# Batch 0 of the first layer: its operands built earlier among its adjacency pieces, and its attention put beside its own preparation

## The chip, the cores and the metric

One Trainium2 chip, one of its cores. The metric is device time in microseconds (us) of one execution of the whole program, from three runs of the kernel before; beside them stands one execution taken by the hardware profiler. The engines of the core are named as in the profile: PE (TensorE) multiplies matrices, DVE (VectorE) and ACT (ScalarE) work element by element, POOL (GpSimd) and SP (SyncE) here mostly issue transfers. Each engine takes its own instructions in a fixed order and waits on semaphores of the others.

## What is computed

Four graph layers over 16 graphs of 1024 nodes with 128 features, each inside `x = layernorm(x + layer(x, adj))`. The change touches only the first layer, for each graph `b`:

```
h       = x @ W.T + W_b                          # 1024 x 128
e       = (h A) h.T ;  e = e + e.T               # 1024 x 1024
att     = softmax(where(adj > 0, e, -9e15), axis=1) * adj
h_prime = relu(att @ h)
c       = sigmoid([x, h_prime] @ gate_w.T + gate_b)
layer   = c * x + (1 - c) * h_prime
```

The later layers (a dilated adjacency with three aggregation steps and batch norms, a second attention, a two-step graph convolution) are not touched.

## The kernel before, in words

The program runs `fast_kernel`; `general_kernel` stands behind a flag for inputs that the fast one does not cover.

**First layer, operands.** The scores are folded: with `M0 = W.T (A + A.T) W` (built from the raw weights at the start, with the column `nu` from the bias), `e` needs only `xT` (x turned, 128 x 1024) and `G = -(M0.T xT) + nu`. `hn` is h by rows, from `xT` and the turned weight `l0WT`. The raw weights (`l0W`, `l0A`, `l0As`, `l0AW`, `l0b`) lie in a pool `l0_raw` on the left side of SBUF; it is closed when `M0` and `nu` exist, and the pool `l0_work`, opened next on the same side, takes over the space. The first tile in it is `xn` of batch 0.

**Preparation, `before(s, b)`.** It loads `xn`, then eight pieces of the adjacency (`it` = 0 to 7), each 128 rows x 1024 (512 KB) into `an`, of which there are three buffers. A piece is cast to fp8 on ACT (the "cast", into `carry`, with the row sums); DVE checks the part right of the diagonal (`chk<-an`); PE turns the blocks up to the diagonal (`pt<-identb,carry`, `it + 1` of them) and DVE compares them with the piece (`chk<-pt,an`), after which the `an` buffer is free. Among the pieces the operands are built: `xT` in the step of piece 2, `G` and the gate part `gx` in that of piece 4, `hn` in that of piece 5. Last, POOL issues the write of the fp8 adjacency to memory (`adj_d<-carry`).

**Attention, `attention(s, b)`.** For each of eight row tiles `jt`: ACT makes the mask (`msk`), PE the scores in two halves (`pmm`, two buffers in PSUM), DVE adds the mask and takes the minimum (`em`, two buffers), ACT takes the exponential with its sum, DVE the reciprocal and the scaled rows `hs`; one round later PE accumulates `acc += hs.T em` in two halves. Row tile `jt` needs the cast of piece `jt` and the columns `jt` of `G`, `xT` and `hn`. Below, e0 stands for the scores of tile 0, acc0 for its accumulation.

**Finish, `after(s, b)`.** Relu, the gate, the mix with x, the layernorm, and the write of x1.

**Order of the work.** The three are generators; `in_rounds` steps those that are due in each round and a `yield n` sets a stream's next turn n rounds on. That fixes the program's order; a scheduler then fixes the order of each engine's queue from it, and may move an instruction ahead of others in the program. In the kernel before, `before(0)` is put in alone; then for each `b` one call of `in_rounds` takes `before(b + 1)`, `attention(b)` and `after(b - 1)` together. The gate bias `gbh` is halved on DVE ahead of all of it.

Of the kernel before, what the change touches and what calls it, by code (L numbers as in the profile page):

```python
# [17 lines left out]
OP = mybir.AluOpType  # L18
# [621 lines left out]
def fast_kernel(ctx: ExitStack, tc: tile.TileContext, t: dict, out: bass.AP, flag: bass.AP):  # L640

    nc = tc.nc
    B, N, D = t["x"].shape
# [43 lines left out]
    def nat(ap):  # L687
        return ap.rearrange("(t p) d -> p t d", p=P)
# [7 lines left out]
    def column(pool, src, name):  # L696
        v = pool.tile([P, 1], F32, name=name)
        nc.sync.dma_start(v, bass.AP(tensor=src.tensor, offset=src.offset, ap=[[1, P], [1, 1]]))
        return v

    def matrix(pool, src, name, bufs=1):
        v = pool.tile([P, P], F32, name=name, bufs=bufs)
        nc.sync.dma_start(v, src)
        return v

    def transposed(pool, psum, src, name, tag="tr"):
        v = pool.tile([P, P], F32, name=name)
        p = psum.tile([P, P], F32, name="wtr", tag=tag)
        nc.tensor.transpose(p, src, identf)
        nc.vector.tensor_copy(v, p)  # L710
        return v
# [103 lines left out]
    def in_rounds(streams):  # L815

        due, r = [0] * len(streams), 0
        while any(streams):
            for i, s in enumerate(streams):
                if s is not None and due[i] <= r:  # L820
                    pause = next(s, 0)
                    if pause == 0:
                        streams[i] = None
                    else:
                        due[i] = r + (pause or 1)
            r += 1

    def symmetric(pool, psum, A, name, tag="tr"):
        As = pool.tile([P, P], F32, name=name)
        p = psum.tile([P, P], F32, name="wtr", tag=tag)  # L830
        nc.tensor.transpose(p, A, identf)
        nc.vector.tensor_add(As, A, p)
        return As
# [57 lines left out]
    ps_a = ending.enter_context(tc.tile_pool(name="l0_pa", bufs=1, space=PSUM, reuse_waits="tile"))  # L891
    ps_h = ending.enter_context(tc.tile_pool(name="l0_ph", bufs=2, space=PSUM, reuse_waits="tile"))

    with tc.tile_pool(name="l0_raw", bufs=1) as raw:
        W0 = matrix(raw, t["L0_gnn_W_w"], "l0W")
        W0T = transposed(wts, ps_h, W0, "l0WT", "h")
        As0 = symmetric(raw, ps_h, matrix(raw, t["L0_gnn_A"], "l0A"), "l0As", "h")
        AW = raw.tile([P, P], F32, name="l0AW")
        p = ps_h.tile([P, P], F32, name="wtr", tag="h")
        nc.tensor.matmul(p, As0, W0, start=True, stop=True)  # L900
        nc.vector.tensor_copy(AW, p)
        M0 = wts.tile([P, P], F32, name="l0M")
        p = ps_h.tile([P, P], F32, name="wtr", tag="h")
        nc.tensor.matmul(p, W0, AW, start=True, stop=True)
        nc.vector.tensor_copy(M0, p)
        nu = wts.tile([P, 1], F32, name="l0nu")
        p = ps_h.tile([P, 1], F32, name="wtr", tag="h")
        nc.tensor.matmul(p, AW, column(raw, t["L0_gnn_W_b"], "l0b"), start=True, stop=True)
        nc.vector.tensor_scalar(nu, p, -1.0, None, op0=OP.mult)
# [6 lines left out]
        nc.sync.dma_start(gw[:, :, 0], t["L0_gnn_gate_w"].rearrange("o (h d) -> d (o h)", d=P))  # L916
    gb = row_bcast(wts, t["L0_gnn_gate_b"], 1, "l0gb")
    gbh = wts.tile([P, 1], F32, name="l0gbh")
    nc.vector.tensor_scalar(gbh, gb, 0.5, None, op0=OP.mult)
    nbig = wts.tile([P, 1], F32, name="l0nbig")  # L920
    nc.vector.memset(nbig, BIG)

    def before(s, b):

        s.xn = work.tile([P, NT, P], F32, name="xn", bufs=3)
        nc.sync.dma_start(s.xn, nat(t["x"][b]))
        yield 1
        for it in range(NT):
            c = b * NT + it
            an = early.tile([P, N], F32, name="an", bufs=3)  # L930
            nc.sync.dma_start(an, t["adj"][b][it * P:(it + 1) * P, :])
            nc.scalar.activation(Y[b][:, it, :], an, AF.Copy, accum_out=deg[:, c:c + 1], saturate=False)  # L932

            chk = early.tile([P, N], FP8, name="chk")
            done = (it + 1) * P
            if done < N:
                nc.vector.scalar_tensor_tensor(chk[:, done:], an[:, done:], 0.0, an[:, done:], op0=OP.is_gt,
                                               op1=OP.not_equal, accum_out=other[:, b, it:it + 1], saturate=False)
            for h in range(it // 4 + 1):
                js = range(4 * h, min(4 * h + 4, it + 1))  # L940
                k = slice(js[0] * P, (js[-1] + 1) * P)
                pt = ps_h.tile([P, 512], F32, name="pt", tag="h")
                for i, jt in enumerate(js):
                    nc.tensor.matmul(pt[:, i * P:(i + 1) * P], Y[b][:, jt, it * P:done], identb, start=True, stop=True)
                nc.vector.scalar_tensor_tensor(chk[:, k], pt[:, :k.stop - k.start], 0.0, an[:, k], op0=OP.is_gt,
                                               op1=OP.not_equal, accum_out=other[:, b, 7 + it + 4 * h:8 + it + 4 * h],
                                               saturate=False)
            if it == 2:
                s.xT = work.tile([P, N], F32, name="xT", bufs=2)
                for p, c, _ in turned(ps_h, s.xn):  # L950
                    nc.scalar.copy(s.xT[:, c], p)
            elif it == 4:
                s.G = work.tile([P, N], F32, name="G", bufs=2)
                for p, c in products(ps_h, (M0, s.xT)):
                    nc.scalar.activation(s.G[:, c], p, AF.Identity, scale=-1.0, bias=nu)
                pz = gates(ps_h, early.tile([P, N], FP8, name="chk").bitcast(F32), (gw[:, 0, :], s.xT))
                s.gx = small.tile([P, NT], F32, name="gx")
                nc.vector.tensor_copy(s.gx.rearrange("p (q t) -> p q t", t=2), pz[:, :, :, 0])
            elif it == 5:
                s.hn = work.tile([P, N], F32, name="hn")  # L960
                for p, c, blocks in halves(ps_h):
                    for i, k in enumerate(blocks):
                        nc.tensor.matmul(p[:, i * P:(i + 1) * P], s.xT[:, k * P:(k + 1) * P], W0T, start=True, stop=True)
                    nc.vector.tensor_add(tiles3(s.hn[:, c]), tiles3(p), b0[:, None, :].to_broadcast([P, 4, P]))
            yield 2
        nc.gpsimd.dma_start(adj8_d[b], Y[b].bitcast(F32))

    def attention(s, b):
        s.acc = ps_a.tile([P, N], F32, name="acc")

        def weigh(jt, hs, em):
            for h in range(H2):
                c = slice(h * 512, (h + 1) * 512)
                nc.tensor.matmul(s.acc[:, c], hs, em[:, c], start=(jt == 0), stop=(jt == NT - 1))  # L974

        for jt in range(NT):
            js = slice(jt * P, (jt + 1) * P)
            c = b * NT + jt
            mn = mx0[:, c:c + 1]
            msk = work.tile([P, N], BF16, name="msk", bufs=2)  # L980
            nc.scalar.activation(msk, Y[b][:, jt, :], AF.Identity, scale=-BIG, bias=nbig)  # L981
            e = wide_matmul(ps_w, s.G[:, js], s.xT)
            em = work.tile([P, N], F32, name="em", bufs=2)
            nc.vector.tensor_tensor_reduce(em, e, msk, 1.0, 3.0e38, op0=OP.add, op1=OP.min, accum_out=mn)  # L984
            sm = small.tile([P, 1], F32, name="sm")
            nc.scalar.activation(em, em, AF.Exp, scale=-1.0, bias=mn, accum_out=sm)  # L986
            rs = small.tile([P, 1], F32, name="rs")
            nc.vector.reciprocal(rs, sm)
            hs = small.tile([P, P], F32, name="hs")
            nc.vector.tensor_scalar(hs, s.hn[:, js], rs, None, op0=OP.mult)  # L990
            yield
            if jt:
                weigh(*late)
            late = jt, hs, em
            yield
        weigh(*late)
        yield
# [23 lines left out]
        yield  # L1021

    state = [Batch() for _ in range(B)]
    in_rounds([before(state[0], 0)])
    for b in range(B):
        streams = []
        if b < B - 1:
            streams.append(before(state[b + 1], b + 1))
        streams.append(attention(state[b], b))
        if b:  # L1030
            streams.append(after(state[b - 1], b - 1))
        in_rounds(streams)
# [225 lines left out]
    with ExitStack() as ph:  # L1258
# [230 lines left out]
        before = None  # L1489
# [5 lines left out]
        for l in range(3):  # L1495
# [42 lines left out]
            before = step  # L1538
# [7 lines left out]
    with ExitStack() as ph:  # L1546
# [7 lines left out]
        W2T, b2, As2, gw, gb, nbig, blcol, Wl = l2.W2T, l2.b2, l2.As2, l2.gw, l2.gb, l2.nbig, l2.blcol, l2.Wl  # L1554
# [247 lines left out]
        state = l2.state  # L1802
# [63 lines left out]
```

## Time and profile before

| what | us |
|---|---|
| three runs, lowest, median, highest | 2731.83, 2735.02, 2736.03 |
| the profiled execution, its own time | 2734.11 |
| its span, first to last instruction | 2732.4 |
| PE, DVE, ACT busy in the span | 2552.2, 2108.6, 1977.0 |
| first layer's attention, first score product to the lull of PE | 28.57 to about 630 |

In the profile L12 is line 12 of the kernel. A line of the timeline gives start, duration, engine, line, operation and `out<-in`, with a count where several were merged, and in brackets the idle time before it and what ended it. SPq and POOLq are the queues from which transfers are issued, and the time shown for one of them is that of the issue; the landing comes later. A matmul line at f32 is counted as two per 512 columns.

### The profile page before, as it was taken

The page shows a single profiled execution, that of the slowest core. Times are in us where ns is not written, and L with a number is a line of the kernel's source. Part 1 is how long each engine was busy: PE and PEld are TensorE (multiplying, and loading weights), DVE is VectorE, ACT ScalarE, POOL GpSimd, SP SyncE. Part 2 cuts the span into 40 slices and gives each one's busy share as a digit, 9 for nine tenths or more (in the row PEclk, how much of TensorE's full clock was granted, in tenths as well). Part 3 has the DMA queues.
Part 4 walks back from the last instruction along what each step waited for, and adds up shares of the span by engine and source line. Part 5 has one row for each costly group of instructions (what it writes and reads, how often), then busy time and mean ns, then how long its engine had stood idle before and what let it go on. Part 6 is the DMA issues. An engine that isn't in the chain of part 4 may idle for free.

```text
span 2732.4 us, 41821 instructions
## 1 busy us (share of the span) xinstructions
PE 2552.2 (93%) x15048; PEld 1688.8 (62%) x15048; DVE 2108.6 (77%) x5650; ACT 1977.0 (72%) x3188; POOL 317.1 (12%) x287
## 2 busy tenths in 40 slices
PE   7999999994899888998999998999999999999986
PEld 3444444442666657887778887456666666666655
DVE  5887778875999986776678877577787787787785
ACT  6888889873888786666655543777777777777773
POOL 0000000003000001121112123001010010001001
PEclk9999999996999999999999999999999999999998
DMA  5455445430000042233356655101222211111100
GB/s 189 162 169 171 165 167 177 157 114 23 2 2 2 2 183 96 94 108 124 132 203 224 254 205 211 39 24 62 70 77 73 90 62 62 62 62 62 46 24 25
DMA packets 120810, 285.38 MB, mean 104 GB/s; under 512 B 12305, under 2 KB 65425, under 8 KB 113425
## 3 DMA queue, kind: packets, MB, share of 16 engines
q1 hardware_dynamic: 101280, 203.33, 22.4%
q0 software_dynamic: 19312, 79.28, 7.5%
q8 instruction: 121, 1.98, 0.3%
q14 instruction: 97, 0.79, 0.1%
HBM read 202.72 MB, written 79.82 MB: 103 GB/s over the span
## 4 chain that ended last, share of the span: by engine, by line
PE 62%; DVE 16%; issue 9%; POOL 5%; ACT 4%; DMA 3%; SPq 0%; POOLq 0%; ACTq 0%; DVEq 0%
PE acc L974 8%; PE ph L1618 8%; PE pmm L724 8%; PE acc L1678 7%; PE ph L766 6%; PE acc L1306 5%; PE ph L759 4%; PE pmm L1690 3%; POOL rn L745 2%; PE ph L1605 2%; PE ph L1432 2%; DVE mid L1097 2%; POOL ln_rstd L745 1%; PE s L1144 1%; DVE keep L1148 1%
## 5 line engine op out<-in xcount | busy, mean ns | idle before, releaser
L745 POOL TENSOR_TENSOR ln_rstd<-ln_rstd,mhalf 128x8 f32<-128x8 f32 (+1 forms) x68 | 108.3, 1592 | 1347.6 <-DVE ln_rstd L742 879.7
L974 PE MATMUL acc<-em,hs 128*128 128x512 f32 x512 | 260.1, 607 | 1.9 <-DVE past L1075 1.3
L724 PE MATMUL pmm<-xT,G 128*128 128x512 f32 x512 | 261.8, 604 | 0.0
L1678 PE MATMUL acc<-ex,hs 128*128 128x512 f32 x512 | 248.9, 596 | 7.4 <-DVE hs L1705 4.5
L801 ACT ACTIVATE xn<-xn,ln_nb,ln_rstd 128x128 f32<-128x128 f32 x512 | 204.6, 481 | 70.3 <-DVE ln_nb L799 70.3
L1306 PE MATMUL acc<-a,lo 128*128 128x512 f32 x768 | 240.4, 398 | 15.3 <-DVE lo L1273 15.3
L1306 PE MATMUL acc<-a,hi 128*128 128x512 f32 x768 | 241.4, 399 | 3.8 <-ACT hi L1272 3.6
L986 ACT ACTIVATE em<-em,mx 128x1024 f32<-128x1024 f32 x128 | 146.4, 1144 | 63.5 <-DVE mx L984 63.0
L1698 ACT ACTIVATE ex<-em,mn 128x1024 f32<-128x1024 f32 x128 | 146.8, 1147 | 44.6 <-DVE mn L1695 43.9
L984 DVE CUSTOM_DVE_ANT_0 em<-pmm,msk 128x1024 f32<-128x1024 f32 x128 | 156.0, 1219 | 27.0 <-PE pmm L724 26.4
L1306 PEld LDWEIGHTS acc<-a,lo 128*128 128x128 f32 x768 | 144.3, 190 | 52.2 <-DVE lo L1273 22.6
L1690 PE MATMUL pmm<-G,hT 128*128 128x512 f32 (+3 forms) x416 | 175.3, 523 | 0.1
L1695 DVE CUSTOM_DVE_ANT_0 em<-pmm,msk 128x1024 f32<-128x1024 f32 x128 | 155.3, 1214 | 24.4 <-PE pmm L1692 22.3
L1306 PEld LDWEIGHTS acc<-a,hi 128*128 128x128 f32 x768 | 144.1, 191 | 34.1 <-ACT hi L1272 4.6
L1157 ACT ACTIVATE carry<-pc,negone 128x1024 fp8e4<-128x1024 f32 x128 | 140.8, 1114 | 27.0 <-PE pc L1156 21.7
L932 ACT ACTIVATE carry<-an 128x1024 fp8e4<-128x1024 f32 x128 | 134.4, 1050 | 21.7 <-DMA an<-in_adj 20.7
L981 ACT ACTIVATE msk<-carry,l0nbig 128x1024 bf16<-128x1024 fp8e4 x128 | 145.4, 1137 | 0.0
L1618 PE MATMUL ph<-A,hi 128*128 128x512 f32 x512 | 143.1, 420 | 1.2 <-DVE zn L1607 0.7
L1686 ACT ACTIVATE msk<-A,nbig 128x1024 bf16<-128x1024 fp8e4 x128 | 144.1, 1136 | 0.0
L1678 PEld LDWEIGHTS acc<-ex,hs 128*128 128x128 f32 x512 | 88.7, 190 | 76.8 <-issue 54.6
L1295 ACT CAST a<-A 128x1024 fp32r<-128x1024 fp8e4 x96 | 99.1, 1050 | 50.9 <-PE acc L1306 50.9
L1295 ACT CAST a<-carry 128x1024 fp32r<-128x1024 fp8e4 x96 | 99.3, 1049 | 47.6 <-PE acc L1306 47.4
(319 smaller groups left out, 6237.4 us busy)
## 6 DMA issues: line engine op xcount, KB each, us to landing
an<-in_adj SPq DMA_DIRECT2D x128, 512.0 KB, 3.6
adj_d<-carry POOLq DMA_DIRECT2D x16, 1024.0 KB, 4.2
A<-dil_d SPq DMA_DIRECT2D x16, 1024.0 KB, 5.6
rdeg<-rdeg_d SPq DMA_DIRECT2D x32, 512.0 KB, 3.8
A<-adj_d SPq DMA_DIRECT2D x16, 1024.0 KB, 4.8
ag_d<-ag POOLq DMA_DIRECT2D x24, 512.0 KB, 5.0
ag<-ag_d SPq DMA_DIRECT2D x24, 512.0 KB, 5.0
xn<-in_x SPq DMA_DIRECT2D x16, 512.0 KB, 4.3
```

What stands on the lines that cost most here:

```text
L724: nc.tensor.matmul(p[:, h * 512:(h + 1) * 512], lhsT, rhs[:, h * 512:(h + 1) * 512], start=True, stop=True)
L745: nc.gpsimd.tensor_tensor(r, r, mhalf[:, :n], op=OP.pow)
L766: nc.tensor.matmul(p, W, x[:, c], start=(i == 0), stop=(i == len(pairs) - 1))
L801: nc.scalar.activation(r[:, k.start + i, :], r[:, k.start + i, :], AF.Identity, scale=rstd[:, i:i + 1], bias=nb[:, i:i + 1])
L974: nc.tensor.matmul(s.acc[:, c], hs, em[:, c], start=(jt == 0), stop=(jt == NT - 1))
L984: nc.vector.tensor_tensor_reduce(em, e, msk, 1.0, 3.0e38, op0=OP.add, op1=OP.min, accum_out=mn)
L1295: nc.scalar.copy(a, A[:, 2 * i:2 * i + 2, c])
L1306: nc.tensor.matmul(acc, part[:, jt, :], pieces[h * NT // 2 + i][:, j, :], start=(jt == 0 and p == 0), stop=(jt == NT - 1 and p == 1))
L1618: nc.tensor.matmul(p, part[:, jt, :], A[jt][:, c], start=(jt == 0 and i == 0), stop=(jt == NT - 1 and i == 1))
L1678: nc.tensor.matmul(s.acc[:, c], hs, ex[:, c], start=(jt == 0), stop=(jt == NT - 1))
L1690: nc.tensor.matmul(e[:, c], s.hT[:, js], s.G[:, c], start=True, stop=True)
L1695: nc.vector.tensor_tensor_reduce(row, e, msk, 1.0, 0.0, op0=OP.add, op1=OP.min, accum_out=mn)
```

## The change

1. The pool of the raw weights goes on the right side of SBUF, so that `l0_work` takes no space from it.
2. For batch 0 alone, `xT` is built in the step of piece 0 (before: piece 2), `G` and `gx` in that of piece 1 (before: 4), `hn` in that of piece 2 (before: 5). For all other batches they stay in the steps of pieces 2, 4 and 5.
3. The first call of `in_rounds` takes `before(0)`, `attention(0)` from round 8 on, and `before(1)` from round 16 on. Piece `it` of batch 0 has its turn in round `1 + 2 it`, tile `jt` of its attention in round `8 + 2 jt`, and piece `it` of batch 1 in round `17 + 2 it`. The loop over `b` then starts with `b = 1`.
4. The instruction that halves the gate bias stands after that first call.

```diff
@@ -891,7 +891,7 @@
-    with tc.tile_pool(name="l0_raw", bufs=1) as raw:
+    with tc.tile_pool(name="l0_raw", bufs=1, side="right") as raw:
...
@@ -916,7 +916,6 @@
     gbh = wts.tile([P, 1], F32, name="l0gbh")
-    nc.vector.tensor_scalar(gbh, gb, 0.5, None, op0=OP.mult)
...
@@ -945,18 +944,18 @@
-            if it == 2:
+            if it == (2 if b else 0):
                 s.xT = work.tile([P, N], F32, name="xT", bufs=2)
...
-            elif it == 4:
+            elif it == (4 if b else 1):
                 s.G = work.tile([P, N], F32, name="G", bufs=2)
...
-            elif it == 5:
+            if it == (5 if b else 2):
                 s.hn = work.tile([P, N], F32, name="hn")
...
@@ -1021,8 +1020,9 @@
     state = [Batch() for _ in range(B)]
-    in_rounds([before(state[0], 0)])
-    for b in range(B):
+    in_rounds([before(state[0], 0), chain([8], attention(state[0], 0)), chain([16], before(state[1], 1))])
+    nc.vector.tensor_scalar(gbh, gb, 0.5, None, op0=OP.mult)
+    for b in range(1, B):
         streams = []
         if b < B - 1:
             streams.append(before(state[b + 1], b + 1))
```

More of the change, by code (lines that the diff above doesn't have):

```diff
@@ L951, in before @@
                     nc.scalar.copy(s.xT[:, c], p)
-            elif it == 4:
+            if it == (4 if b else 1):
                 s.G = work.tile([P, N], F32, name="G", bufs=2)
```

## Prediction

> **What bounds the kernel now.** I read the page's slices first, then a table of busy time by stretch, then the timeline of the first 45 us, then the waits of the transfer queue.
>
> ```profile
> span 2732.4 us, 41821 instructions
> PE   7999999994899888998999998999999999999986
> DVE  5887778875999986776678877577787787787785
> ACT  6888889873888786666655543777777777777773
> ```
>
> The first layer fills slices 0 to 8 of 68.3 us each. PE is at 9 in all but the first, so this stage ends when PE has done its work, and what counts at the head is how long PE stands idle. By stretch (columns: length, then busy PE, PEld, DVE, ACT, POOL, clock, DMA share, GB/s):
>
> ```profile
> 0.00:14.00 14.00, 3.28 (x12) 2.32 (x13) 5.13 (x30) 6.68 (x9) 1.08 (x8) 1.00 0.40 131
> 14.00:29.00 15.00, 9.18 (x35) 4.38 (x33) 5.70 (x20) 6.09 (x13) 0.00 (x0) 1.00 0.87 275
> 29.00:45.00 16.00, 14.74 (x71) 7.71 (x70) 12.91 (x39) 11.04 (x19) 0.71 (x1) 1.00 0.60 203
> 45.00:60.00 15.00, 15.00 (x68) 7.47 (x67) 10.21 (x37) 14.56 (x26) 0.00 (x0) 1.00 0.45 143
> 300.00:400.00 100.00, 100.00 (x425) 49.62 (x424) 82.25 (x274) 90.47 (x156) 9.15 (x9) 1.00 0.51 170
> ```
>
> PE idles 10.7 + 5.8 + 1.3 = 17.8 us up to 45 us, and then not at all (later rows are like the last). ACT at 90% and DVE at 82% have slack. So a microsecond of PE idleness saved in the head is a microsecond of the program. Why is PE idle?
>
> ```profile
> 7.04 0.15 DVE L919 TENSOR_SCALAR l0gbh<-l0gb 128x1 f32<-128x1 f32 x1 [4.13 <-DMA l0gb<-in_L_gnn_gate_b]
> 8.46 1.09 DVE L937 SCALAR_TENSOR_TENSOR chk<-an 128x896 fp8e4<-128x896 f32 x1 [1.27 <-DMA an<-in_adj]
> 10.98 0.27 DVE L832 TENSOR_TENSOR l0As<-l0A,wtr 128x128 f32<-128x128 f32 x1
> 13.53 0.38 SPq L926 DMA_DIRECT2D xn<-in_x  x1
> 17.88 1.94 PE L759 MATMUL ph<-identf,xn 128*128 128x128 f32 x8 [3.08 <-DMA xn<-in_x]
> 23.85 3.78 PE L766 MATMUL ph<-xT,l0M 128*128 128x512 f32 x4 [0.95 <-DVE chk L945]
> 28.57 1.14 PE L724 MATMUL pmm<-xT,G 128*128 128x512 f32 x2
> ```
>
> DVE's constants queue behind the first piece's check, so l0As is late; xn is issued only when the raw weights' space is free; xT, G and the first scores follow in a chain. Once attention runs, the engines pace one another:
>
> ```profile
> 37.90 1.06 ACT L932 ACTIVATE carry<-an 128x1024 fp8e4<-128x1024 f32 x1 [3.25 <-DMA an<-in_adj]
> 38.96 1.13 ACT L986 ACTIVATE em<-em,mx 128x1024 f32<-128x1024 f32 x1
> 40.09 1.13 ACT L981 ACTIVATE msk<-carry,l0nbig 128x1024 bf16<-128x1024 fp8e4 x1
> 42.60 1.22 DVE L984 CUSTOM_DVE_ANT_0 em<-pmm,msk 128x1024 f32<-128x1024 f32 x1
> ```
>
> A piece that lands late stops ACT. The waits of SP's own queue to 60 us (in all, times, longest) and the transfers' time to landing say why it may:
>
> ```profile
> SPq L931 <- DVE chk L945: 51.5, 15, 12.8
> SPq L926 <- DVE l0AW L901: 6.9, 1, 6.9
> DMA to landing us min/median/max: 3.4/4.7/5.8
> ```
>
> Three an buffers; each new load waits for DVE's last check of an old piece, then takes 4.7 us.
>
> **What the Trainium skill says.** *PSUM — Partial Sum Buffer*, section "Engine vs sequencer instructions": engine queues are strict FIFO, matmuls complete in program order. The trace agrees: xn's wait held the an loads behind it to 14.34. *DMA: Bandwidth & Descriptors*, "Anatomy of one DMA — SWDGE (gpsimd) path": about 2.0 us fixed plus bytes over 436 GB/s, an estimate of 3.2 us for 512 KB; the trace's 4.2 for xn (13.53 to 17.8) and 4.7 for an are longer, on SP's queue, and I use those. *TensorE: Matmul & The Clock Gate*, "What's actually happening": PE runs at half rate until busy for some 3.4 us. The trace agrees in kind: the four M0 products take 3.78 us at 23.85 and 1.94 us at 51.65, though the clock column says 1.00 at both.
>
> **The change, part by part.** I walk the built instruction order of the changed kernel with durations above. Pace (start to start) is what queues up: cast 1.05, exp 1.13, mask 1.04, em 1.14; on PE scores 1.72 and accumulation 1.77 per tile, hn 1.8.
>
> *Raw pool, loads.* In the built order SP issues xn of batch 0 at the place of the first an (4.14), then three an, then xn of batches 1 and 2, then piece 3. xn lands at about 8.4. The three an follow at 9.7, 11.0, 12.3: before, they landed from 8.4 on, and 1.3 us is 512 KB at the 418 GB/s seen from 8 to 10 us. So the pieces pay 1.3 us. The extra xn loads (2.6 us) delay nothing: piece 3's load waits for the check of piece 0 (12.8) and lands near 17.2, and its cast is due at 18.3.
>
> *gbh.* The scheduler puts it back where it was on DVE, waiting to 7.04. Value 0; bounds 0 to 0.15 either way.
>
> *M0.* The constants now precede the first check: l0As at 7.19 + (10.98 - 9.48) = 8.7. But that check (9.7 to 10.75) stands ahead of l0AW, so M0 comes at 12.2, not 13.6.
>
> *xT, G, first scores.* Turns of xn 12.3 to 14.25 (as slow as before), one slot of piece 1, M0 products from 14.6: 3.78 us if cold, 1.94 if warm. PE has by then been nearly continuously busy since 11.1, so I take 3.0; gate products 0.8; first scores at 18.4 (bounds 17.4 and 19.4), 10.2 us before 28.57. PE has done 9.4 us of work by then (3.0 up to M0, from the 3.28 of the first row; 0.7 for the turns of pieces 0 and 1; 1.9; 3.0; 0.8): 9.0 us idle.
>
> *What is late next.* At 28.57 the old kernel had six casts and five pieces' checks done; the new one at 18.4 has three and two. The rest now shares ACT and DVE with attention. New waits, by queue:
> - DVE: em of tile 0 waits for e0 (20.2); behind it the check of piece 2, done at 23.0. SP's load of piece 5 waits for that: issued 23.1, landed 27.5 (4.4 us; ends 3.4 and 5.8). Its cast fits just in time.
> - Piece 3's check, behind em of tile 1 and both halves of hn, ends at 26.95: piece 6 lands at 31.45. ACT has nothing in front of that cast from 28.55, and exp of tile 2 is queued behind it. On PE the turns of piece 6 wait, with acc1's second half behind: **1.5 us idle**.
> - acc7 waits for hs of tile 7, behind exp7 and DVE's checks of pieces 3 and 4 of batch 1: **1.0 us**.
> - The gate turns of batch 1 wait for ACT's copy, behind the cast of piece 6 and the relu: **1.0 us**.
> - Small ones (piece 5, acc5): 0.3. POOL's 1 MB write, freed by cast 7 at about 34.8 instead of 31.5, now meets the loads of batch 1's pieces 1 and 2; 0.5 for that (0 to 2; it is not free, for nothing hides a late cast here). Nothing waits for POOL itself; further on its x1 write goes ahead of the next batch's adjacency write, with no reader near: 0.
>
> Sum after 18.4: 4.3 us. The alone stretch of batch 1's pieces 4 to 7, which the rounds suggest, costs nothing more: the built order fills it with batch 1's scores, G and hn.
>
> *Sum.* Idle PE after: 9.0 + 4.3 = 13.3, against 17.8: **4.5 us saved**. Cross-check by content: the walk has e0 of batch 1, acc7 and the gate turns done at 61.7 + 0.5; the old trace reaches that content at 70.95 less 3.2 us of work further on (hn and two pieces' turns), 67.75: 5.5 us. From batch 3 on the orders are the same, PE is full in both, and the rest moves as one. Profiled: 2734.1 - 4.5 = 2729.6 (span 2732.4 to 2727.9, 1.7 around it). The median of the runs is 0.9 above the profiled execution: 2735.0 - 4.5 = **2730.5**.
>
> **Rivals.**
> *A, the stalls are hidden.* PE turns warm early and loads land in 3.4 us, so only about 1.3 us of idleness is left, as in 29 to 45 now: with scores at 17.4, 8.0 + 1.3 = 9.3 idle, 8.5 saved, 2726.5. For: the page's min of 3.4; PE is busy on end from 11.1. Against: a median of 4.7 with the same number of loads in flight.
> *B, slower: the ring of three an buffers behind in-order DVE.* Every piece from 5 of batch 0 to 4 of batch 1 (8 of them) stalls PE as piece 6 does. At 5.8 us to landing, 1.4 more than I took, each adds 1.4 x 8 = 11.2 idle: 13.3 + 11.2 = 24.5, 6.7 slower, 2741.7. It decides from 4.5 / 8 = 0.6 us extra per piece, that is from 5.0 us to landing. For: ACT already waited 3.25 us for one piece. Against: after piece 6 the walk has most loads landing before ACT reaches their cast.
> *C, nothing.* The gain is eaten on the way to batch 3, PE waits up to 17.8 in sum: 2735. For: ACT at 90% has to catch up three casts. Against: its slack of 10% is 3 us per 30.
> That the change does not do what it says is excluded by the built order: xn heads the loads and scores come before piece 2's turns.
>
> **How the numbers follow.** A measurement of this kernel tells about 0.2% (5.5 us) from no change, so my 4.5 sits just inside. Main forecast 0.50 (2728 to 2733); A 0.24; C 0.16; B 0.10. Faster by over 0.2%: A and a third of the main case (0.18): 0.42. Slower: most of B, with a little of C: 0.10. Same: 0.48. Range 2725.5 to 2737: A's end and a little under it, and C with the runs' spread, leaving out B and tails.
>
> **What would show it.** First scores (pmm) near 18.4 and the M0 products near 14.6; xn issued at about 4.1; piece 6's cast with a wait for its load near 31 and PE idle before its turns; PE's idle sum to 65 us near 13.3. Wrong if first scores come after 21, if idle PE appears past 70 us, or if loads take over 5.0 us.

## The result and the profile after

| | kernel before | changed kernel |
|---|---|---|
| median of the runs (lowest to highest) | 2733.41 (2730.95 to 2736.03), 9 runs | 2726.49 (2723.03 to 2730.03), 9 runs |
| the profiled execution, its own time | 2734.11 | 2723.06 |
| its span | 2732.4 | 2721.3 |

The ratio is 0.9976, with a 95% interval of 0.9966 to 0.9985: the median of the changed kernel is 6.9 us lower (4.1 to 9.3 by the interval). The forecast was 2730.5, 4.5 us faster. In the runs of the experiments below, one execution of e3_alone, of 3651.69 us at a granted clock of 0.66, is left out. The two profiled executions differ by more, 11.1 us in span. So there are two questions: is the head's gain what the steps said, and where does the rest come from?

The page's first line and three rows of its slices, in the kernel after:

```profile
span 2721.3 us, 41812 instructions
PE   8999999994899889998999998999999999999986
DVE  6788777875999986776678877577877878787785
ACT  7888889873888786666655544777777777777773
```

PE's first slice is at 8 where it was at 7, and DVE and ACT are busier in slice 0. By stretch (length, then busy PE, PEld, DVE, ACT, POOL, clock, DMA share, GB/s):

```profile
0.00:14.00 14.00, 4.50 (x16) 3.29 (x17) 6.04 (x32) 4.86 (x8) 1.08 (x8) 1.00 0.70 216
14.00:29.00 15.00, 14.54 (x68) 7.67 (x67) 8.58 (x29) 12.54 (x19) 0.00 (x0) 1.00 0.47 137
29.00:45.00 16.00, 15.35 (x58) 6.86 (x56) 13.83 (x42) 13.31 (x22) 0.71 (x1) 1.00 0.78 258
45.00:60.00 15.00, 13.43 (x52) 6.14 (x51) 6.21 (x22) 13.61 (x22) 0.00 (x0) 1.00 0.42 139
300.00:400.00 100.00, 100.00 (x416) 49.77 (x415) 79.57 (x263) 90.08 (x156) 9.49 (x9) 1.00 0.53 172
```

Length less busy PE gives 9.50, 0.46, 0.65 and 1.57 us of idle PE, and the rows after these add 0.84 (60 to 75 us), 0.55 (90 to 105) and 0.47 (120 to 200). The sum is 14.0, where the kernel before had 17.8. The stretch of 14 to 29 us was 5.8 idle and is now almost full; 45 to 60 was full and now is not. The timeline shows the start of the chain:

```profile
4.14 0.43 SPq L925 DMA_DIRECT2D xn<-in_x  x1
7.10 0.15 DVE L1024 TENSOR_SCALAR l0gbh<-l0gb 128x1 f32<-128x1 f32 x1 [4.15 <-DMA l0gb<-in_L_gnn_gate_b]
8.67 0.28 DVE L832 TENSOR_TENSOR l0As<-l0A,wtr 128x128 f32<-128x128 f32 x1
10.10 1.09 DVE L936 SCALAR_TENSOR_TENSOR chk<-an 128x896 fp8e4<-128x896 f32 x1 [1.15 <-DMA an<-in_adj]
12.73 1.96 PE L759 MATMUL ph<-identf,xn 128*128 128x128 f32 x8
15.36 3.08 PE L766 MATMUL ph<-xT,l0M 128*128 128x512 f32 x4 [0.46 <-ACT xT L950]
18.94 1.98 PE L724 MATMUL pmm<-xT,G 128*128 128x512 f32 x4
```

xn is issued 9.4 us sooner, PE has no idle time just ahead of xn's turns (they now follow the weights' small products and the turn of piece 0), and the first scores start at 18.94 instead of 28.57. The main waits of ACT and PE after that:

```profile
30.97 1.06 ACT L931 ACTIVATE carry<-an 128x1024 fp8e4<-128x1024 f32 x1 [2.60 <-DMA an<-in_adj]
33.97 1.06 ACT L931 ACTIVATE carry<-an 128x1024 fp8e4<-128x1024 f32 x1 [0.72 <-DMA an<-in_adj]
35.17 0.23 PE L943 MATMUL pt<-identb,carry 128*128 128x128 bf16 x1 [0.56 <-ACT carry L931]
52.72 0.22 PE L943 MATMUL pt<-identb,carry 128*128 128x128 bf16 x1 [0.57 <-DVE chk L944]
53.94 1.12 PE L766 MATMUL ph<-xT,l0M 128*128 128x512 f32 x2 [1.00 <-DVE chk L944]
68.32 1.06 ACT L931 ACTIVATE carry<-an 128x1024 fp8e4<-128x1024 f32 x1 [2.34 <-DMA an<-in_adj]
69.53 0.23 PE L943 MATMUL pt<-identb,carry 128*128 128x128 bf16 x1 [0.84 <-ACT carry L931]
101.42 1.10 PE L973 MATMUL acc<-em,hs 128*128 128x512 f32 x2 [0.55 <-DVE hs L989]
```

How much of the head's gain survives is read from marks. POOL's power of `ln_rstd` belongs to a batch's normalisation, after its attention: for batch 0 it starts at 92.68 before and 88.24 after (4.4 us sooner), for the fourth at 205.30 and 200.71 (4.6), for the fourteenth at 580.45 and 576.12 (4.3). The first instruction after the first layer that both kernels have on POOL is the power of the degrees. Before:

```profile
627.96 20.73 POOL L1183 TENSOR_TENSOR deg<-deg,mhalf 128x128 f32<-128x128 f32 x1 [5.87 <-DVE deg L1182]
```

and after:

```profile
623.52 20.74 POOL L1183 TENSOR_TENSOR deg<-deg,mhalf 128x128 f32<-128x128 f32 x1 [5.87 <-DVE deg L1182]
```

The lead at this mark, called the degree mark below, is **4.44 us**. Up to 992 us the two traces keep it within 0.3 us. It then grows to 11.1 at 1848 us, in a stage whose instructions are the same in both, and stays there to the end.

### The profile page after: what moved, and what is told of

Its sections match the earlier page's. It is cut to its first block, busy times and chain, and to the rows that moved or that the text cites. A ratio compares the mean times of both kernels' runs of the same rounds, so it can differ in the third digit from the quotient of the medians.

```text
span 2721.3 us, 41812 instructions
## 1 busy us (share of the span) xinstructions
PE 2547.0 (94%) x15048; PEld 1683.6 (62%) x15048; DVE 2108.4 (77%) x5650; ACT 1977.4 (73%) x3188; POOL 317.0 (12%) x287
## 4 chain that ended last, share of the span: by engine, by line
PE 58%; DVE 17%; issue 7%; POOL 5%; ACT 5%; DMA 2%; POOLq 0%; ACTq 0%; DVEq 0%; SPq 0%
PE ph L1618 8%; PE acc L1678 7%; PE acc L973 6%; PE pmm L724 6%; PE acc L1306 6%; PE ph L766 6%; PE ph L759 3%; PE pmm L1690 3%; PE ph L1605 2%; POOL rn L745 2%; PE ph L1432 2%; POOL ln_rstd L745 2%; DVE mid L1097 1%; ACT q L1145 1%; PE s L1144 1%
```

## The experiments

Two theories were put to the test. The first: the head's gain is less idle PE, because xn is there early and xT and G are made beside the first pieces. Its rivals: the order of the rounds makes the gain, or ACT's pace at the pieces hides all of it, or (the prediction's slower rival) the ring of three an buffers decides. The second: what the profiled pair shows beyond 4.4 us is a matter of where the TensorE clock's half-rate windows fall. Its rival: the change shortens the later stage too.

All times are in us; "idle" is the sum of PE's idle time to 400 us; the medians are of runs made together, with the kernel before run beside them on the same chip. First scores, idle time and mark are those of one profiled execution each.

| run | first scores | idle | degree mark | median, kernel before | ratio, 95% interval |
|---|---|---|---|---|---|
| before | 28.57 | 17.8 | 627.96 | | |
| changed | 18.94 | 14.0 | 623.52 | 2726.49, 2733.41 | 0.9976 (0.9966 to 0.9985) |
| after_again | 19.83 | 14.7 | 624.56 | 2725.29, 2731.18 | 0.9979 (0.9970 to 0.9989) |
| e1_left | 24.90 | 18.5 | 629.14 | 2732.55, 2732.39 | 0.9998 (0.9990 to 1.0006) |
| e2_right | 26.15 | 15.0 | 626.03 | 2730.39, 2732.39 | 0.9991 (0.9983 to 0.9999) |
| e3_alone | 18.92 | 14.4 | 626.08 | 2725.68, 2732.39 | 0.9967 (0.9954 to 0.9980) |
| e4_late_ops | 25.87 | 18.7 | 628.89 | 2732.04, 2732.39 | 0.9996 (0.9990 to 1.0003) |
| e9_m0 | 19.30 | 13.4 | 623.46 | 2730.47, 2732.45 | 0.9992 (0.9983 to 1.0001) |
| e10_xt | 20.09 | 13.7 | 624.50 | 2730.15, 2732.45 | 0.9990 (0.9984 to 0.9997) |
| e11_dve | 17.85 | 12.3 | 622.85 | 2724.96, 2731.18 | 0.9976 (0.9964 to 0.9987) |
| e6_an4 | 20.40 | 13.7 | 621.19 | 2725.50, 2732.45 | 0.9978 (0.9968 to 0.9988) |
| e12_dve4 | 19.00 | 11.1 | 620.32 | 2724.21, 2731.18 | 0.9973 (0.9962 to 0.9984) |
| e7_an2 | 18.75 | 31.2 | 665.85 | 2765.24, 2732.45 | 1.0119 (1.0103 to 1.0134) |

The two executions of the changed kernel show what one reading is worth: 18.94 and 19.83 for the first scores, 14.0 and 14.7 idle, 623.52 and 624.56 at the mark. A difference of about 1 us between two kernels is therefore not read as an effect. Idle time saved and lead at the mark agree within 1.0 us in all runs but three: e3_alone, e6_an4 and e7_an2, which are taken up below.

**e1_left: the raw weights back on the left side.**

```diff
-    with tc.tile_pool(name="l0_raw", bufs=1, side="right") as raw:
+    with tc.tile_pool(name="l0_raw", bufs=1) as raw:
```

> The changed kernel, but the raw weights stay on the left side, where xn's space is only free after they are used. Theory (the gain is PE idleness saved in the head, and the early xn is its first cause): xn is issued near 13.5 us again instead of 4.14, its turns start near 17.9 and the M0 products near 20, first scores at 22 to 24 instead of 18.94; three to four of the 4.4 us of lead that the changed kernel has at the degree reciprocal (line 1183: 623.52 against 627.96) are lost, so that mark lies at 626.5 to 627.5; idle PE up to 75 us near 17. Rival (the order of the rounds alone carries the gain): the mark stays at 623.5 to 624.5. Second theory, on the other 6.7 us of the profiled pair: the time from this mark to the end follows the microseconds that the clock record shows at half clock there (20.5 before, 6.8 after) at half a microsecond each, whatever the head does; its rival: the time after the mark is set by the order of the head.

The timeline of this kernel:

```profile
13.57 0.38 SPq L925 DMA_DIRECT2D xn<-in_x  x1
17.82 1.94 PE L759 MATMUL ph<-identf,xn 128*128 128x128 f32 x8 [3.84 <-DMA xn<-in_x]
24.90 1.12 PE L724 MATMUL pmm<-xT,G 128*128 128x512 f32 x2
```

xn is late again. The first scores come later than expected (24.90, not 22 to 24), and the mark is not some 1 us better than before, as the theory had it, but 1.2 us worse; the medians are equal to 0.2 us. Without the early xn the rest of the change gives nothing, although its scores still start 3.7 us sooner than before. The rival, that the order of the rounds alone carries the gain, is out. Earlier scores alone are thus no gain; idle PE is 18.5. (The 20.5 and 6.8 us at half clock in the expectation are what is left without the windows that both executions have in the same places. From the mark to the end it is 130.1 and 116.4 in all; the difference of 13.7 is the same.)

**e2_right: the kernel before, with only the raw weights on the right side.**

```diff
-    with tc.tile_pool(name="l0_raw", bufs=1) as raw:
+    with tc.tile_pool(name="l0_raw", bufs=1, side="right") as raw:
```

> The kernel before, with only the raw weights moved to the right side. Theory: xn is issued near 4.1 us and lands near 8.4, but xT and G keep their place at pieces 2 and 4 and attention its place behind the preparation, so first scores come at 26 to 28.6 against 28.57, and the degree mark at 626 to 628 (lead 0 to 2). Rival (the early xn carries the gain): lead 3.5 to 4.5, mark at 623.5 to 624.5. For the rest of the time: half a microsecond per microsecond at half clock after the mark, as in the other runs.

```profile
4.14 0.43 SPq L926 DMA_DIRECT2D xn<-in_x  x1
21.43 3.78 PE L766 MATMUL ph<-xT,l0M 128*128 128x512 f32 x4 [0.76 <-DVE chk L945]
26.15 1.30 PE L724 MATMUL pmm<-xT,G 128*128 128x512 f32 x2
```

xn comes at the same 4.14 as in the changed kernel, but the products of G have kept their place among the pieces and start at 21.43. The lead is 1.9 at the mark, where that rival asked for 3.5 to 4.5, and 2.0 in the medians (0.3 to 4.6 by the interval). So the early xn by itself is a part of the gain, about half of it or less, and by the mark not all of it.

**e4_late_ops: the changed kernel with xT, G and hn at pieces 2, 4, 5, and attention from round 12.**

```diff
-            if it == (2 if b else 0):
+            if it == 2:
...
-            if it == (4 if b else 1):
+            if it == 4:
...
-            if it == (5 if b else 2):
+            if it == 5:
...
-    in_rounds([before(state[0], 0), chain([8], attention(state[0], 0)), chain([16], before(state[1], 1))])
+    in_rounds([before(state[0], 0), chain([12], attention(state[0], 0)), chain([16], before(state[1], 1))])
```

> The changed kernel with xT, G and hn of batch 0 back at pieces 2, 4 and 5, attention from round 12 on. Theory (G beside piece 1 is what brings the scores forward): M0 products at 21 or later, first scores at 23 to 26, lead at the degree mark 0.5 to 2.5. Rival (only the right side and the interleaving count, ACT's pace at the pieces hides the rest): lead 3.5 to 4.5. After the mark: half a microsecond per microsecond at half clock.

```profile
21.84 3.53 PE L766 MATMUL ph<-xT,l0M 128*128 128x512 f32 x4 [0.95 <-DVE chk L944]
25.87 1.12 PE L724 MATMUL pmm<-xT,G 128*128 128x512 f32 x2
103.67 1.96 PE L973 MATMUL acc<-em,hs 128*128 128x512 f32 x4 [1.59 <-DVE hs L989]
```

(In the kernel the second of these tests is an `if`, not the `elif` printed with the change; since the tests exclude each other, it does the same.) The scores are late, as expected, but no lead is left at all: the mark is 0.9 behind the kernel before, where 0.5 to 2.5 ahead was expected, and the medians are equal to 0.4 us. PE's idle time from 75 to 400 us is 2.6, where the kernel before has none; the stall at 103.67 is a part of it. With e1_left this says that both halves are needed for the whole gain: xn early, and xT and G beside the first pieces.

**e3_alone: the changed kernel with the rounds as before.**

```diff
-    in_rounds([before(state[0], 0), chain([8], attention(state[0], 0)), chain([16], before(state[1], 1))])
+    in_rounds([before(state[0], 0)])
+    in_rounds([before(state[1], 1), attention(state[0], 0)])
```

> The changed kernel with the rounds as before: batch 0's preparation runs out alone, then attention of batch 0 beside batch 1's preparation; xT, G and hn stay beside pieces 0, 1 and 2, the raw weights on the right. Theory (operands early make the gain; in the built order the scheduler then pulls the first scores forward by itself, and its order at the head is nearly the changed one): first scores at 19 to 20, mark at 623.5 to 624.5, lead 3.5 to 4.5. Rival (the interleaved rounds carry the gain): first scores at 24 or later, lead under 2. After the mark: half a microsecond per microsecond at half clock.

First scores come at 18.92 without the interleaved rounds: the scheduler moves them ahead of the later pieces by itself. The mark in the profile missed (626.08, where 623.5 to 624.5 was expected). PE's timeline and the row of 45 to 60 us show the larger part of why:

```profile
43.94 0.23 PE L943 MATMUL pt<-identb,carry 128*128 128x128 bf16 x1 [2.30 <-ACT carry L931]
45.91 1.92 PE L724 MATMUL pmm<-xT,G 128*128 128x512 f32 x2
45.00:60.00 15.00, 15.00 (x56) 7.21 (x56) 8.64 (x29) 13.58 (x25) 0.56 (x1) 0.89 0.33 105
```

PE waits 2.30 us for the cast of a late piece. Right after that the trace's clock record has a window of 3.4 us at half clock, from 44.8 to 48.2 us, and the two score products in it take 1.92 us instead of 1.08. Half of 3.4 us, an estimate of what the window costs, is 1.7 of the 2.6 us by which this mark lies behind the changed kernel's. The profiled execution took 2731.66, the longest of the five; the median is 6.7 below the kernel before, like the changed kernel's. So the rounds, the edit that looks largest in the diff, were not needed for the gain in the runs. How much of it this kernel keeps at the mark in a typical execution was not seen.

**e9_m0 and e10_xt: the remaining idle PE ahead of the scores.** In e9_m0 ACT halves the gate bias, and DVE's checks of the pieces go behind `nu`:

```diff
-        nc.vector.tensor_scalar(nu, p, -1.0, None, op0=OP.mult)
+        made = nc.vector.tensor_scalar(nu, p, -1.0, None, op0=OP.mult)
...
-                nc.vector.scalar_tensor_tensor(chk[:, done:], an[:, done:], 0.0, an[:, done:], op0=OP.is_gt,
-                                               op1=OP.not_equal, accum_out=other[:, b, it:it + 1], saturate=False)
+                with tc.issue_after(made.ins):
+                    nc.vector.scalar_tensor_tensor(chk[:, done:], an[:, done:], 0.0, an[:, done:], op0=OP.is_gt,
+                                                   op1=OP.not_equal, accum_out=other[:, b, it:it + 1], saturate=False)
...
-    nc.vector.tensor_scalar(gbh, gb, 0.5, None, op0=OP.mult)
+    nc.scalar.activation(gbh, gb, AF.Identity, scale=0.5)
```

> The changed kernel with the halved gate bias made on ACT and DVE's check of the first piece put behind nu, so that nothing of DVE's waits ahead of the weights' small products. Theory (what is left idle before the first scores is M0's chain behind gbh and the first check: l0As 8.67, l0AW 11.12, M0 12.29): M0 near 9 to 10, and xn's turns are then bound by PE's order behind the turns of piece 0 and by the landing at 8.4; first scores at 16.5 to 18.5 instead of 18.94, degree mark 0.5 to 2 us before the changed kernel's 623.52. Rival (first scores are bound by the transfer of xn and ACT's copies anyway): first scores at 18.5 to 19.5, mark within 0.5 us of 623.52. The runs' median moves by the same amount, within 2.5 us for the half-clock windows after the mark.

e10_xt is e9_m0, with batch 0's xT ahead of its loop of pieces:

```diff
+        if not b:
+            s.xT = work.tile([P, N], F32, name="xT", bufs=2)
+            for p, c, _ in turned(ps_h, s.xn):
+                nc.scalar.copy(s.xT[:, c], p)
         yield 1
...
-            if it == (2 if b else 0):
+            if b and it == 2:
```

> The kernel of the run before this one, with batch 0's xT made ahead of the loop of pieces, so that PE turns xn ahead of piece 0. Theory (idle PE ahead of the first scores is what the head costs): M0 products at 12 to 13.5, first scores at 15.5 to 17, idle PE to 14 us 8.5 to 9, and the degree mark 1.5 to 3.5 us before the changed kernel's 623.52. Rival (from here on the pieces' loads set the pace, and scores that come sooner only wait longer at pieces 4 to 7): first scores as early, but idle PE of 14 to 45 us grows by what was saved, and the mark stays within 1 us of 623.52.

Both missed on the first scores: 19.30 and 20.09, no sooner than the changed kernel's 18.94 and 19.83, although M0 is there at 6.9 and 7.1 instead of 12.3. The timeline of e10_xt:

```profile
7.28 0.16 DVE L909 TENSOR_SCALAR l0nu<-wtr 128x1 f32<-128x1 f32 x1
8.72 1.94 PE L759 MATMUL ph<-identf,xn 128*128 128x128 f32 x8 [1.47 <-DMA xn<-in_x]
14.20 1.05 ACT L929 COPY xT<-ph 128x512 f32<-128x512 f32 x2
15.47 3.78 PE L766 MATMUL ph<-xT,l0M 128*128 128x512 f32 x4
```

M0 and nu are ready at 7.4 and xn is turned at 10.7, but ACT has three casts and a mask ahead of the copies of xT, which end at 15.25. After the hole of 4 us that this leaves on PE the products take 3.78 instead of 3.08, at half rate to their end. So bringing M0 forward did not bring the scores forward; the copies in ACT's queue set them. Both marks, 623.46 and 624.50, lie within 1 us of the changed kernel's, as the rivals had it. The runs' medians are only 2.0 and 2.3 below the kernel before, where the changed kernel's are 5.9 and 6.9 below; at like marks, so the head does not explain that, and nothing here does.

**e11_dve: e10_xt with DVE copying batch 0's xT and G.**

```diff
-                nc.scalar.copy(s.xT[:, c], p)
+                nc.vector.tensor_copy(s.xT[:, c], p)
...
-                    nc.scalar.activation(s.G[:, c], p, AF.Identity, scale=-1.0, bias=nu)
+                    if b:
+                        nc.scalar.activation(s.G[:, c], p, AF.Identity, scale=-1.0, bias=nu)
+                    else:
+                        nc.vector.tensor_scalar(s.G[:, c], p, -1.0, nu, op0=OP.mult, op1=OP.add)
```

> The kernel with xT ahead of the pieces, with batch 0's copies of xT and G on DVE, where ACT had them behind three casts and a mask. Theory (once xn is early, what sets the first scores is the queue of the engine that copies): M0 products at 12 to 13.5 instead of 15.47, first scores at 16 to 17.5 instead of 20.09, degree mark 1 to 3 us before the changed kernel's 623.52. Rival (the ring of three an buffers sets the pace afterwards): first scores as early, mark within 1 us of 623.52, the idle PE moved to 29 to 75 us.

```profile
11.17 1.28 DVE L929 COPY xT<-ph 128x512 f32<-128x512 f32 x2
13.66 3.69 PE L766 MATMUL ph<-xT,l0M 128*128 128x512 f32 x4
17.85 1.13 PE L724 MATMUL pmm<-xT,G 128*128 128x512 f32 x2
```

The products start 1.7 us sooner than in the changed kernel and 1.8 sooner than in e10_xt, the scores 1.1 and 2.2, which bears out that ACT's queue was in the way; both come a little later than expected. Idle PE falls by 1.8 against the changed kernel; at the mark 0.7 is left (1.7 against its second execution), within what two executions of one kernel differ by. The rival's mechanism is not seen: the idle time did not move to 29 to 75 us, where it is 3.0 against 3.1.

**e6_an4: four an buffers.** (A small tile of the normalisation has one buffer less, to make room.)

```diff
-            an = early.tile([P, N], F32, name="an", bufs=3)
+            an = early.tile([P, N], F32, name="an", bufs=4)
```

> The changed kernel with four an buffers instead of three (one small tile of the normalisation has one buffer less, to make room). Theory (casts of pieces 6 and 7 wait 2.6 and 0.7 us for loads that could not be issued before an old piece's check had freed its buffer): these waits vanish, idle PE of 29 to 75 us falls from 3.1 to about 1 us, the mark lies 0.5 to 2 us before 623.52. Rival (the loads share the transfer engines, so one more in flight lands as late): waits for an stay, mark within 0.5 us; or later by up to 1.5 us, since a fourth load at the start delays the xn of batch 0 or the pieces.

The mark is 2.3 us sooner than in the changed kernel (3.4 against its second execution), a little over the expected range, but not for the reason given. Four loads go out ahead of xn, the scores come 1.5 us later, ACT's waits for an from 20 to 75 us do not vanish (7.5 us against 6.2), and PE's idle time of 29 to 75 us is 2.4, not about 1. The groups of PE's instructions up to 10.6 us before the mark say where the time is (count, then busy us, mean ns, idle before it). The turns of the pieces, changed kernel:

```profile
L943 PE MATMUL pt<-identb,carry 128*128 128x128 bf16 x576 | 65.0, 220 | 2.4 <-ACT carry L931 1.4 <-DVE chk L944 0.6 <-DVE l0M L905 0.2
```

and with four buffers:

```profile
L943 PE MATMUL pt<-identb,carry 128*128 128x128 bf16 x576 | 59.9, 220 | 1.0 <-DVE chk L944 0.6 <-ACT carry L931 0.3 <-DVE l0M L905 0.2
```

576 turns of 220 ns take 65.0 us of PE in one and 59.9 in the other, because more of them follow each other closely and overlap. Since turns also overlap the matmuls of other groups, the group's 5.1 is not all gained: PE's busy time in all falls by 2.0 (598.9 to 596.9 up to that point), its idle time by 0.3, and the two make the 2.3 at the mark. So most of this gain is not visible as idle time. Why the turns lie closer together with four buffers was not followed up. In the runs the gain is not seen: the median is 7.0 below the kernel before, the changed kernel's 6.9 and 5.9.

**e7_an2: two an buffers.**

```diff
-            an = early.tile([P, N], F32, name="an", bufs=3)
+            an = early.tile([P, N], F32, name="an", bufs=2)
```

> The changed kernel with two an buffers instead of three, to price the rival that the ring of an behind DVE's in-order checks is what could have made the change slower. If that ring is as tight as the rival had it, each of the 64 pieces of the first layer waits some 1.5 to 4 us at its cast, and PE idles in all of the first layer: 60 us or more slower. If it is loose (only pieces 5 to 7 of batch 0 and the first of batch 1 feel it): 3 to 12 us slower at the degree mark. If the ring does not matter: within 1 us of 623.52.

The mark is 42.3 us later than the changed kernel's, between the two sizes expected, and the runs are 32.8 above the kernel before. (The first layer has 128 pieces, not the 64 of the expectation.) The row of 300 to 400 us, full in the kernel before and in the changed one:

```profile
300.00:400.00 100.00, 93.30 (x373) 45.18 (x374) 72.06 (x228) 81.38 (x138) 7.84 (x8) 0.97 0.45 154
```

ACT waits 33.0 us for pieces between 82 and 620 us, where the changed kernel waits 12.7. Up to 10.6 us before the mark PE is idle for 24.3 us more than in the changed kernel and busy for 18.0 more; 13.7 us at half clock, in four windows, make an estimated 6.8 of the latter. The slower rival's mechanism is real and one buffer away, but with three buffers it did not take hold.

**e12_dve4: e11_dve with four an buffers, and the first four an loads kept behind xn** (`got` is the load of xn; the small tile of the normalisation as in e6_an4).

```diff
-            an = early.tile([P, N], F32, name="an", bufs=3)
-            nc.sync.dma_start(an, t["adj"][b][it * P:(it + 1) * P, :])
+            an = early.tile([P, N], F32, name="an", bufs=4)
+            if c < 4:
+                with tc.issue_after(got.ins):
+                    nc.sync.dma_start(an, t["adj"][b][it * P:(it + 1) * P, :])
+            else:
+                nc.sync.dma_start(an, t["adj"][b][it * P:(it + 1) * P, :])
```

> The run before this one with four an buffers, and the first four an loads kept behind xn. If both the start and the ring cost: first scores at 15.5 to 17 and the mark at 617.5 to 620.5, 3 to 6 us before the changed kernel and 0.5 to 3.5 before the run with four buffers alone (621.19); runs 8 to 12 us below the kernel before. If the ring alone counts: mark at 620.7 to 621.7. If four loads in flight delay the pieces: later than 621.7.

```profile
13.06 2.08 PE L766 MATMUL ph<-xT,l0M 128*128 128x512 f32 x2 [0.96 <-DVE chk L953]
15.98 2.08 PE L766 MATMUL ph<-xT,l0M 128*128 128x512 f32 x2 [0.74 <-DVE G L966]
19.00 1.59 PE L724 MATMUL pmm<-xT,G 128*128 128x512 f32 x2
```

The scores missed: DVE's queue, now with the copies and the checks, holds both halves of the products, which run at half rate (2.08 us each, where one takes 1.12 at 53.94 in the changed kernel). The mark is in the range all the same, 3.2 us before the changed kernel's, so the ring of buffers counts. It is 0.9 before e6_an4's, too little to say that the start counts beside it. The median, 7.0 below the kernel before, misses the 8 to 12 expected; it is the lowest of all, but the interval doesn't tell it from the changed kernel's (5.9 below the same runs).

**after_again: the changed kernel once more.**

> The changed kernel once more, unaltered, for the 2.5 us between the medians' difference (6.9) and the lead at the degree mark (4.4). Theory (that remainder is chance: where the free-running half-clock windows of 3.4 us fall after the mark): the mark is at 623 to 624 again, but the time from mark to end differs from the 2097.8 of the first profile by one to several times 1.7 us, with other windows, and the median of the runs lies between 2726 and 2730, nearer to 4.4 below the kernel before. Rival (the change also shortens the later stage): median at 2725 to 2727.5 again, and 2097 to 2099 from mark to end.

The mark is 1.0 later, at 624.56, a little outside what was expected (first scores at 19.83). The time from there to the end is 2101.5 against 2097.8, with other windows, as the theory had it: the same program varies by 4.8 us in its profiled span. But the median, 2725.29, lies in the rival's range and not in the theory's, at 5.9 below the kernel before, and so again 2.5 more than the lead of this execution's mark, 3.4. This run alone does not decide between the two.

**The later stage.** Take the stretch from POOL's `rdeg_d` near 1213 us to the `ln_rstd` near 1840, with the same instructions in all 13 profiled executions, and the microseconds in it that the trace's clock record shows at half clock, always in multiples of 3.413:

| | at half clock | length |
|---|---|---|
| changed, e6_an4, e12_dve4 | 17.1 | 624.3, 624.9, 625.8 |
| e11_dve, e7_an2 | 20.5 | 627.7, 627.4 |
| e4_late_ops, e2_right | 23.9 | 625.7, 631.8 |
| after_again, e10_xt, e9_m0, e3_alone, e1_left | 27.3 | 628.0, 628.6, 630.4, 630.6, 630.7 |
| before | 30.7 | 630.5 |

A line through the 13 points rises by 0.41 us per microsecond at half clock (correlation 0.78), and the points lie up to 3.5 us off it; without the profiled pair it rises by 0.39 (correlation 0.71). Between the pair that is 13.7 x 0.41 = 5.6 of the 6.2 us by which this stretch differs. Over the whole time from the mark to the end it is less clear: 0.27 per microsecond (correlation 0.64), where the expectations had a half. That the windows are free-running is what the Trainium skill says in *TensorE: Matmul & The Clock Gate*, "What's actually happening" (3413 ns, not reset by the kernel's start); the records agree, since within one execution all windows lie on one grid of 3.413 us, and its offset differs between the two executions of the changed kernel (0.54 and 1.89 us after a multiple, from the start of the span).

That the change itself shortens this stretch is not seen: e9_m0 and e3_alone, whose heads have the same early xn and operands, take 630.4 and 630.6 there, as long as the kernel before, and the changed kernel's first execution is the shortest of the 13. So the extra 6.7 us of the profiled pair are put down mostly to chance; that the windows are the cause is argued from the correlation, since no experiment shifted them. The medians' extra 2.5, in both sets of runs of the changed kernel, lies within their intervals and stays open. Other medians do not follow the marks either: e9_m0, with the same mark, is only 2.0 below the kernel before.

## Why the prediction held, step by step

The forecast difference of 4.5 us lies inside the measured interval (4.1 to 9.3) and next to the lead at the mark. The median itself, 2726.49, lies 4.0 under the forecast 2730.5, below the main forecast's 2728 to 2733 and inside the whole range. Of the 4.0, 1.6 is the kernel before, whose median over nine runs is 2733.41 where the forecast started from 2735.02 over three; the other 2.4 is the part that stayed open above. And the prediction gave a difference under 0.2% the better chance (0.48 to 0.42), where the ratio shows 0.24%.

- **PE bounds the first layer, so idle PE saved is time saved.** Held: 17.8 - 14.0 = 3.8 idle saved, 4.44 of lead at the mark (forecast 4.5). It is a rule to within a microsecond or so, not an identity: e6_an4 saved 4.1 of idle time and gained 6.8, by turns that overlap more.
- **xn at 4.14, M0 at 12.2, products at 14.6, scores at 18.4.** xn issued at 4.14; the pieces 0.4 later than forecast (first check at 10.10, 9.7 in the walk); M0 at 12.29, since l0AW was copied at 11.12, behind the check of the first piece in DVE's queue, as the walk had it; turns at 12.73 instead of 12.3; products at 15.36, 0.8 late: 0.4 from the turns, the rest because the copy of xT on ACT (0.46 of wait) was not in the walk. They took 3.08, where 3.0 was a value chosen between 3.78 and 1.94. That it fitted is in part luck: the clock record begins, at full clock, at 17.60 us, in the midst of the products, and in the second execution at 18.96, where they took 3.54. A clock of 1.00 shown ahead of this first entry says nothing. Scores at 18.94. Idle PE until then is 9.5 + 0.46 = 10.0, where the walk had 9.0.
- **gbh: nothing.** It waits to 7.10 as before.
- **What is late next: 4.3 us.** The sum is near (14.0 - 10.0 = 4.0), the places are mostly not. Up to 65 us, where the walk ended, only 2.2 came: PE was idle for 12.2 us by then, where 13.3 was forecast. The other 1.9 came at 69.53 and later, where the walk had nothing. The cast of piece 6 did wait for its load, until 30.97 (31.45 forecast), but PE had other work and lost nothing there; 0.56 came at piece 7. The 1.0 for acc7 and the 1.0 for the gate turns did not occur. In their place PE waited 1.57 at 52.7 to 54.0 for DVE's checks of batch 1, and 0.84 at 69.53 for a cast behind a load. A sum of terms that miss in both directions came out near the measured one, which is luck as much as method.
- **From batch 3 on the rest moves as one.** Held for the first layer, 4.3 to 4.6 of lead at every batch's mark from the fourth; idle PE past 70 us, which the prediction named as a sign that it is wrong, did appear (1.0 us). The marks of the second and third batch are only 3.8 and 3.4 sooner; from the fourth on nothing is lost. Beyond the first layer it failed: the lead of the profiled pair grows to 11.1, and two executions of one kernel differ there by 3.7.
- **Rival A** (2726.5) is where the median came, but not by its mechanism: idle PE is 14.0, not 9.3, and the scores are at 18.94, not 17.4. **Rival B** needed over 5.0 us to landing; the median of an up to 60 us is 4.2 (longest 7.0), and e7_an2 shows what it looks like when it does decide. **Rival C**, nothing left by batch 3: out, with 4.6 of lead there.

## What to carry to other kernels

When a chain at the start is shortened by an earlier load, ask at once which in-order queue its next step stands in: here the copy on ACT, behind casts, and after that DVE's, took back most of what further edits gave. A small gain in one stage is better judged by a mark at that stage's end than by the total, as long as the total has a later stage that varies by itself from run to run; but profile the same kernel twice, for the mark varies too (1.0 us here). And try the parts alone: the early load gave about half of the gain or less, the early operands without it none, and the reordered rounds were not needed.

## What was not expected of the hardware

The same program differs by 4.8 us between two profiled executions, 3.7 of it in one stretch of some 630 us in which PE drops to half clock for 17.1 us in one and 27.3 us in the other. And four products of the same shape at the head took 3.08 and 3.54 us in the two executions of the changed kernel, 3.78 in e10_xt, and 4.16 in two halves with a wait between them in e12_dve4; 1.94 further on in the kernel before. The clock records account for it: their first entry, at full clock, comes at 17.60, 18.96, 19.93 and 19.98 us, in the midst of the products in the first two and after their end in the others. At the pace of 3.78 us for all four up to that moment and of 1.94 after it, an estimate gives 3.0 and 3.5 us for the first two. Last, a wait of PE shorter than a window can be followed by a window at half clock: 2.30 us in e3_alone ahead of the one at 44.8, and 1.97 us in e7_an2 ahead of one at 71.6.
